# Four-layer graph attention: in the second layer, VectorE adds two of four weighted rows in every third group, and TensorE sums three

## The chip, the cores and the metric

The kernel runs on one core of a Trainium2 chip. The metric is the device time of one execution in microseconds, the median over several runs. In this text PE is TensorE, DVE is VectorE, ACT is ScalarE, POOL is GpSimd, and SP is the engine that issues plain DMAs.

## What is computed

There are 3327 nodes with 512 features each, and a sparse symmetric adjacency matrix (each node has some 17 neighbours on average, itself included). Four attention layers follow each other. Each one normalises the rows, applies a rectifier, projects with a 512 x 512 weight, and takes for every node the mean of its neighbours' projected rows, weighted by a softmax over the neighbours. The result is added to the input of the layer. The second layer has four heads of 128 features:

```python
def _L1_gnn_ref(H, A, W, a_l, a_r):
    mask = A + jnp.eye(n, dtype=A.dtype) > 0
    Wh = (H @ W).reshape(n, N_HEADS, D_K)
    sl = jnp.einsum('nhd,hd->nh', Wh, a_l)
    sr = jnp.einsum('nhd,hd->nh', Wh, a_r)
    e = jax.nn.leaky_relu(sl[:, :, None] + sr.T[None, :, :], negative_slope=NEG_SLOPE)
    e = jnp.where(mask[:, None, :], e, -jnp.inf)
    alpha = jnp.nan_to_num(jax.nn.softmax(e, axis=2), nan=0.0)
    out = jnp.einsum('nhm,mhd->nhd', alpha, Wh).reshape(n, OUT_DIM)
    return jax.nn.elu(out)
...
h = jnp.maximum(_layernorm(x, axis=-1), 0.0)
x = x + _L1_gnn_ref(h, adj, L1_gnn_W, L1_gnn_a_l, L1_gnn_a_r)
```

Layers 1 and 4 have eight heads, layer 3 has one. All arithmetic that matters here is in float32.

## The kernel before

The kernel first turns the adjacency matrix into lists of neighbours, ranks the nodes by their number of neighbours, and works on 26 tiles of 128 nodes in that order. `CAPS[t]` is the longest list in tile t: 36 for tile 0, 25 for tile 1, then falling to 11 for tile 25. Nodes with long lists (in the second layer, tile 0 alone; `DENSE`) are handled by dense products over the whole mask (class `Several`), spread over the same steps as the rest. This happens for each layer in turn; in code the second layer has `l == 1`.

For the other tiles (class `Tile`), the neighbours' rows are fetched in groups of four (`GROUP`). A tile with K neighbours has K/4 groups, rounded up, and the last group can be shorter. A group goes through these stages:

- `fetch`: POOL issues one indirect DMA for each of the four rows (L834). It takes 128 rows of the projected table from DRAM into one of seven buffers `g`. The first row of a tile is the nodes' own and comes by a plain DMA from SP (L865).
- `scored`: VectorE adds the two score terms and applies the leaky rectifier (z, L887 and L889), ScalarE takes the exponential into `pw` (L890).
- `group`: VectorE multiplies each of the four rows by its weights, head by head, into a buffer `m` (L916; three such buffers). TensorE then adds the rows up in a PSUM bank: each row is multiplied by the identity matrix and accumulated (L921), from the tile's first row to its last.

When a tile's last group is done, `finish` puts its epilogue in later steps: `divisors` and `means` on VectorE (L926 to L938), the ELU (`bent` on ScalarE at L944 and L946, `added` on VectorE at L952 and L958), then the variance (L966 and L969 on ScalarE, L974 and the root at L434 to L440 on VectorE), the transposes (L450), the projection for the next layer (L468), and the store of the projected rows (L475 on ScalarE, L992 on SP).

Everything is in program order: the outer loop runs over steps, one group each, and each engine executes its instructions in the order in which the loop writes them. In step s the order is: what is due "first" (a part of the dense work, transposes), then `scored` of group s + 1, what is due at "scored", then `group` of step s, then what is due "last". Tiles run from 25 down to 1.

Of the kernel before, what the change touches and what calls it, by code (L numbers as in the profile page):

```python
# [35 lines left out]
GROUP = 4  # L36
# [759 lines left out]
def tile_gat_lists(ctx: ExitStack, tc: tile.TileContext, x, adj, ws, avs, out, ident, half, slots, L, low, spare, tabx, tabs):  # L796
# [7 lines left out]
    nc = tc.nc  # L804
# [40 lines left out]
    class Tile:  # L845
# [51 lines left out]
        def group(self, i):  # L897


            H, K, wt = HEADS[self.l], CAPS[self.t], self.wt  # L900
            D = F // H
            k0, n, g = self.groups[i]
            if H == 1:
                for q in range(n):
                    v = g[:, q, :].rearrange("p (s m) -> p s m", s=2)[:, :, :F // 2]
                    acc = self.po.rearrange("p (s m) -> p s m", s=2)
                    w = wt[:, k0 + q, 0:1]
                    if k0 + q == 0:
                        nc.vector.tensor_scalar(acc, v, w, None, OP.mult)
                    else:  # L910
                        nc.vector.scalar_tensor_tensor(acc, v, w, acc, OP.mult, OP.add)  # L911
                return
            m = pools["m"].tile([P, GROUP, F], F32, name="m")
            for q in range(n):
                v = g[:, q, :].rearrange("p (s m) -> p s m", s=2)[:, :, :F // 2]
                nc.vector.tensor_tensor(m[:, q, :].rearrange("p (s h d) -> p s h d", s=2, d=D),  # L916
                                        v.rearrange("p s (h d) -> p s h d", d=D),
                                        wt[:, k0 + q, :H].rearrange("p (s h) -> p s h", s=2)
                                        .unsqueeze(3).to_broadcast([P, 2, H // 2, D]), OP.mult)
            for q in range(n):  # L920
                nc.tensor.matmul(self.po, ident, m[:, q, :], start=(k0 + q == 0), stop=(k0 + q == K - 1))  # L921

        def divisors(self):
            H, K = HEADS[self.l], CAPS[self.t]
# [420 lines left out]
    for l in range(NL):  # L1345
# [3 lines left out]
        with ExitStack() as c2:  # L1349
# [39 lines left out]
            for s in range(-1, at_end):  # L1389
# [10 lines left out]
                if 0 <= s < len(steps):  # L1400
                    tl, i = steps[s]
# [55 lines left out]
```

## Time and profile before

| | us |
|---|---|
| median of three runs without the profiler (2468.46 to 2473.81) | 2471.52 |
| the profiled execution's own time | 3002.17 |
| its span, first to last instruction | 3000.4 |

| stage of the profiled execution | from, to (us) | PE busy | DVE busy | ACT busy | POOL busy |
|---|---|---|---|---|---|
| lists and first projection | 0, 319 | 206.65 | 247.25 | 180.84 | 232.20 |
| layer 1 | 319, 1137 | 600.90 | 461.69 | 180.26 | 469.23 |
| layer 2 | 1137, 1850 | 552.88 | 439.62 | 197.21 | 369.40 |
| layer 3 | 1850, 2312 | 349.23 | 363.80 | 169.94 | 290.16 |
| layer 4 | 2312, 3000 | 530.86 | 398.97 | 185.64 | 388.29 |

The stages are cut where the first and last summing matmuls of a layer lie. A row of the profile names the line, the engine, the operation, output and inputs, the number of instructions, their busy time and the mean duration of one, then the idle time of that engine ahead of them and what ended it. The matmuls' durations overlap, so their sum isn't the time that the engine needs.

### The profile page before, as it was taken

The numbers are of one execution on the slowest core, as the hardware profiler recorded it, in microseconds if no ns is written. First come the engines' busy times: TensorE is split into PE (matmuls) and PEld (weight loads), VectorE is DVE, ScalarE is ACT, GpSimd is POOL, SyncE is SP. The second block draws the span as 40 slices with busy tenths as digits, with TensorE's granted clock in tenths as the row PEclk, the third lists the DMA queues.
The fourth block names the chain that finished last, engine by engine and source line by source line (L and its number), as shares of the span: only waits on it lengthen the run. The fifth ranks groups of instructions, "written<-read, shape, count | busy, mean of one in ns | idle before, by whom it ended". The sixth has DMA issues, their size and how long they took to land. (4 is left out here: it accounts for less than half of the span.)

```text
span 3000.4 us, 26820 instructions
## 1 busy us (share of the span) xinstructions
PE 2240.5 (75%) x6832; PEld 1225.4 (41%) x6832; DVE 1911.3 (64%) x5004; ACT 913.9 (30%) x2506; POOL 1749.3 (58%) x1739
## 2 busy tenths in 40 slices
PE   4777677777767756778778787679796677888787
PEld 2664243443334333444434344345354343444443
DVE  7887656655555545557665564697887456666655
ACT  5782122322221112323232222343333223332220
POOL 7894455565556646454556562676663556565654
PEclk9888888998899888889988888899898788898988
DMA  6885576786676677666766663787784667676664
GB/s 232 309 294 162 163 221 200 212 253 205 189 206 192 199 186 209 181 177 179 200 183 196 181 186 105 236 247 229 218 253 123 202 187 206 182 202 192 202 171 122
DMA packets 262490, 599.55 MB, mean 200 GB/s; under 512 B 103923, under 2 KB 121331, under 8 KB 257974
## 3 DMA queue, kind: packets, MB, share of 16 engines
q0 software_dynamic: 126128, 438.08, 49.7%
q1 hardware_dynamic: 132454, 152.86, 16.1%
q10 hardware_dynamic: 3744, 6.82, 0.7%
q8 instruction: 55, 0.90, 0.1%
q14 instruction: 109, 0.89, 0.1%
HBM read 547.96 MB, written 49.65 MB: 199 GB/s over the span
## 5 line engine op out<-in xcount | busy, mean ns | idle before, releaser
L921 PE MATMUL bank<-m,ident 128*128 128x512 f32 x2608 | 1328.8, 657 | 376.6 <-DVE m L916 218.1
L916 DVE TENSOR_TENSOR m<-g,pw 128x512 f32<-128x512 f32 x1304 | 811.1, 682 | 539.0 <-ACT pw L890 254.4
L834 POOL DMA_INDIRECT g<-tab,idxb x734 | 698.5, 952 | 482.2 <-issue 200.9
L921 PEld LDWEIGHTS bank<-m,ident 128*128 128x128 f32 x2608 | 528.0, 210 | 1038.3 <-issue 646.6
L468 PE MATMUL pv<-w,hT 128*128 128x264 f32 x1664 | 437.7, 418 | 80.0 <-ACT hT L457 45.5
L834 POOL DMA_INDIRECT g<-tabx,twiceb x342 | 324.2, 948 | 248.4 <-issue 153.7
L834 POOL DMA_INDIRECT g<-tab,idxa x297 | 283.0, 953 | 231.1 <-issue 95.6
L468 PEld LDWEIGHTS pv<-w,hT 128*128 128x128 f32 x1664 | 335.9, 206 | 182.5 <-ACT hT L457 52.3
L890 ACT ACTIVATE pw<-z 128x32 f32<-128x32 f32 (+4 forms) x362 | 69.1, 191 | 801.6 <-DVE z L889 442.5
L1146 PE MATMUL whole<-ve,em 128*128 128x512 f32 x468 | 230.1, 644 | 52.0 <-issue 21.8
L694 POOL TENSOR_TENSOR key<-a,keys 128x3328 int32<-128x3328 int32 (+1 forms) x29 | 189.4, 6534 | 16.2 <-DVE cand L703 12.6
L911 DVE SCALAR_TENSOR_TENSOR bank<-g,L,bank 128x512 f32<-128x512 f32 x243 | 183.3, 754 | 11.8 <-remote 3.9
L1146 PEld LDWEIGHTS whole<-ve,em 128*128 128x128 f32 x468 | 94.2, 207 | 164.7 <-issue 124.3
L834 POOL DMA_INDIRECT g<-tabx,twicea x99 | 94.4, 954 | 105.6 <-issue 55.5
L703 DVE MAX8 cand<-key 128x8 f32<-128x208 int32 x416 | 143.9, 364 | 0.1
L450 PE MATMUL pt<-ident,xn 128*128 128x128 f32 x416 | 71.4, 300 | 95.6 <-ACT xn L966 48.4
L475 ACT ACTIVATE v<-pv,rstd 128x528 f32<-128x528 f32 x78 | 54.1, 694 | 265.9 <-remote 118.6
L1271 ACT ACTIVATE spare<-room,low 128x64 f32<-128x64 f32 x208 | 57.9, 337 | 191.7 <-remote 82.2
L450 PEld LDWEIGHTS pt<-ident,xn 128*128 128x128 f32 x416 | 55.6, 155 | 137.8 <-ACT xn L966 54.9
L887 DVE TENSOR_TENSOR z<-g,pw 128x32 f32<-128x32 f32 (+4 forms) x362 | 63.1, 174 | 73.2 <-DMA g<-tab,idxa 43.3
L457 ACT ACTIVATE hT<-pt 128x512 f32<-128x512 f32 x104 | 61.4, 590 | 153.8 <-remote 85.1
L1260 ACT ACTIVATE r<-low,spare 128x256 f32<-128x256 f32 x208 | 98.9, 476 | 10.2 <-remote 2.3
(180 smaller groups left out, 2189.4 us busy)
## 6 DMA issues: line engine op xcount, KB each, us to landing
a<-in_adj SPq DMA_DIRECT2D x25, 1664.0 KB
tab<-v SPq DMA_DIRECT2D x78, 264.0 KB
ve<-tab SPq DMA_DIRECT2D x78, 264.0 KB
g<-tab SPq DMA_DIRECT2D x66, 264.0 KB
tabx<-vx SPq DMA_DIRECT2D x26, 528.0 KB
g<-tab,idxb POOLq DMA_INDIRECT x734
low<-tab SPq DMA_DIRECT2D x52, 132.0 KB
room<-tab SPq DMA_DIRECT2D x52, 132.0 KB
```

Source lines behind the costliest of these rows:

```text
L450: nc.tensor.transpose(pt[:, k, :], xn[:, k * P:(k + 1) * P], ident)
L468: nc.tensor.matmul(pv[:, s, :HF + 8], hT[:, k, :], W.w[:, k, s, :], start=(k == 0), stop=(k == KC - 1))
L694: nc.gpsimd.tensor_tensor(key[:, c:c + quarter], a[:, c:c + quarter], keys[:, c:c + quarter], OP.mult)
L703: nc.vector.max(cand[:, g * 8:(g + 1) * 8], key[:, g * SEG:(g + 1) * SEG])
L834: nc.gpsimd.indirect_dma_start(out=out_, out_offset=None, in_=table, in_offset=bass.IndirectOffsetOnAxis(ap=which, axis=0))
L887: nc.vector.tensor_tensor(z, g[:, :n, ROW - 8:ROW - 8 + H], self.s.unsqueeze(1).to_broadcast([P, n, H]), OP.add)
L890: nc.scalar.activation(self.wt[:, k0:k0 + n, :H], z, AF.Exp)
L911: nc.vector.scalar_tensor_tensor(acc, v, w, acc, OP.mult, OP.add)
L916: nc.vector.tensor_tensor(m[:, q, :].rearrange("p (s h d) -> p s h d", s=2, d=D), v.rearrange("p s (h d) -> p s h d", d=D), wt[:, k0 + q, ...
L921: nc.tensor.matmul(self.po, ident, m[:, q, :], start=(k0 + q == 0), stop=(k0 + q == K - 1))
L1146: nc.tensor.matmul(tl.po.rearrange("p (s m) -> p s m", s=2), e[:, q * P:(q + 1) * P], v.rearrange("p (s m) -> p s m", s=2)[:, :, :F // 2], ...
L1260: nc.scalar.activation(self.r[:, h, :], self.a[:, g, :], AF.Relu, bias=-1.0, scale=self.b[:, j, g:g + 1])
```

## The change

In the second layer, in a group of four rows whose number i in its tile is divisible by three, VectorE adds the second weighted row to the first in place, and TensorE leaves out the matmul of the second. The matmul of the first row then takes the sum of both. In all other groups nothing changes, nor does the order of the steps.

```diff
@@ def group(self, i):
+            pair = self.l == 1 and n == GROUP and i % 3 == 0
+            if pair:
+                nc.vector.tensor_add(m[:, 0, :], m[:, 0, :], m[:, 1, :])
             for q in range(n):
-                nc.tensor.matmul(self.po, ident, m[:, q, :], start=(k0 + q == 0), stop=(k0 + q == K - 1))
+                if not (pair and q == 1):
+                    nc.tensor.matmul(self.po, ident, m[:, q, :], start=(k0 + q == 0), stop=(k0 + q == K - 1))
```

The changed kernel has the same line numbers up to L919, and five more from L921 on.

## The prediction

> **What bounds the kernel now.** I looked first at the span and the time of the profiled execution: span 3000.4 us, time 3002.17 us, against a median of 2471.52 us without the profiler. The profiled execution is 531 us (21%) longer than the runs that count, so everything below is summed against 3002 us, and I have to ask for each stall whether it exists in the undisturbed runs. The split by stage (the busy time of each engine in windows cut where each layer's first and last `bank` matmuls lie) gives for the second layer:
>
> ```profile
> core 0: us, PE busy (x) PEld busy (x) DVE busy (x) ACT busy (x) POOL busy (x), PEclk, DMA share, GB/s
> ...
> 1137.00:1850.00 713.00, 552.88 (x1575) 291.33 (x1574) 439.62 (x1187) 197.21 (x594) 369.40 (x391) 0.89 0.62 178
> ```
>
> PE has 553 of 713 us, VectorE 440; no engine is full. The groups of lines in that window show the work:
>
> ```profile
> L921 PE MATMUL bank<-m,ident 128*128 128x512 f32 x855 | 431.4, 652 | 137.7 <-DVE m L916 115.9 <-issue 20.2 <-DVE z L889 1.1
> ...
> L916 DVE TENSOR_TENSOR m<-g,pw 128x512 f32<-128x512 f32 x423 | 263.1, 682 | 84.1 <-ACT pw L890 49.0 <-remote 17.4 <-issue 10.4
> ...
> L408 DVE TENSOR_TENSOR prod<-w,av 128x512 f32<-128x512 f32 x8 | 5.5, 688 | 0.0
> ```
>
> PE's idle time ahead of the summing matmul ends 116 us with the arrival of a product from VectorE. Why is the product late? The waits of VectorE in this window, longest first:
>
> ```profile
> DVE bank L952 <- ACT ex L946: 71.0, 10, 12.7
> DVE ve L974 <- ACT waste L969: 56.2, 16, 11.6
> DVE m L916 <- ACT pw L890: 49.0, 71, 6.7
> ```
>
> These are some ten microseconds at a time, about once in each tile; I counted 32 gaps over 0.8 us with 210 us in them, and 39 us of short round trips to ScalarE. In the list of waits ScalarE, which works in order, is stuck at the same moments on loads (L1271 <- remote, 53.8 us) while gathers fill the DMA queues. I take it that much of the 531 us that the profiler adds lies in such stalls. So the stretch that best resembles the undisturbed run is one without them, and the stage's end, where all gathers have landed:
>
> ```profile
> 1384.00:1428.00 44.00, 40.78 (x126) 22.38 (x126) 36.71 (x99) 18.09 (x60) 23.99 (x26) 0.96 0.65 187
> ...
> 1812.00:1837.00 25.00, 25.00 (x67) 12.56 (x66) 19.55 (x50) 5.21 (x13) 0.00 (x0) 0.93 0.10 33
> ```
>
> There PE is busy 93% and 100% of the time, VectorE 83% and 78%, and VectorE's remaining gaps are mostly the 0.25 to 0.31 us after each exponential. Over the stage VectorE needs 440 + 39 = 479 us in order. For PE, whose matmuls overlap (eight of L921 take 3.60 us in the timeline, so 0.43 us each and 0.86 us for a weighted row, which is two instructions), the sum is 431 rows x 0.86 = 371, the projection 25 x 3.72 = 93, the dense products 50 x 0.61 = 31, the transposes 25 x 0.60 = 15: 510 us at full clock. POOL's 391 gathers at 1.25 us from start to start are 489 us. Three engines within 7% of each other: none bounds the stage alone.
>
> **What the Trainium skill says.** "VectorE: DVE Perf Modes", section "The TRN2 errata", prices an fp32 tensor_tensor add at (N+151)/0.96 ns, 691 ns at N = 512; the trace agrees (L408, the same shape with both inputs in SBUF: 688 ns). "Perfetto Trace Analysis", section "Per-instruction lifecycle", says that TensorE's end times are estimates; hence I use the spacing 0.43 us and not the 652 ns of the row. "TensorE: Matmul & The Clock Gate", part 1, says the clock is full or half and falls after idle windows; the stage's mean is 0.89, and starts 0.85 us apart stand in the first layer at about 1016 us. "GPSIMD Engine Reference", section 1, says GpSimd's SBUF interfaces are contended by VectorE instructions with two SBUF inputs; the new add is one. No row of the trace before isolates this.
>
> **The change, part by part.** Tiles 1 to 25 of the second layer have 431 rows in 118 groups. A group with four rows and i of 0 or 3 qualifies (6 never has four rows): 25 first groups and 16 fourth ones, 41 in all.
>
> Removed on PE: 41 rows x 2 instructions x 0.43 us = 35.3 us at full clock, 39.6 us at the mean clock 0.89. No DMA, no other engine's instruction goes. The accumulation's first and last matmul stay (q = 0 and q = 3).
>
> Added on VectorE: 41 adds. Alone 0.69 us; in a run of like instructions they start 0.60 us apart (four products take 2.48 us), and one that waits for another starts at that one's end. 41 x 0.62 = 25.4 us taken, bounds 41 x 0.60 = 24.6 and 41 x 0.73 = 29.9. The order of instructions shows the add behind the fourth product, with a wait on VectorE's own earlier products. Queued behind it are the next instructions of the step: the scores z of the next group, or on i = 3 the variance chain (L974, L434 to L440). ScalarE's next exponential waits for z, and POOL's gathers wait for buffers that VectorE frees: each may move by 0.62 us. The release of the group's own gather buffer comes with the products and doesn't move.
>
> Moved: the matmul on q = 0. It now waits for the add. Before, it could start after the first product. In the timeline of tile 24, group 0:
>
> ```profile
> 1145.14 2.48 DVE L916 TENSOR_TENSOR m<-g,pw 128x512 f32<-128x512 f32 x4 [3.22 <-ACT low L1272]
> ...
> 1145.89 3.70 PE L921 MATMUL bank<-m,ident 128*128 128x512 f32 x8 [0.85 <-issue]
> ```
>
> PE starts 0.75 us after VectorE. With the add the products end at 1147.63, the add at about 1148.25, so PE starts at 1148.3 instead of 1145.9: 2.4 us later, with 0.86 us less to do. **Here PE is 1.56 us later after the change, not 0.86 us earlier.** The point from which a group gains is plain: PE has to be behind the end of the fourth product by 0.68 us anyway. I paired the starts of products and matmuls of all 118 groups in the timeline. Of the 41 affected, 27 have PE waiting for the first product (sum +42 us of PE lateness), 8 are in between (+5 us), and 6 are fully covered (6 x -0.86 = -5.2 us). Of the other 77 groups only 15 have PE waiting. The first group of a tile follows a short last group of the one before, and the fourth follows a stall, so the condition i % 3 == 0 picks the groups where PE is hungry. That lateness isn't all lost: it moves into PE's next idle time (160 us in the stage). It does mean that the 35 us saved fall mostly into idle time.
>
> The sum, against the profiled execution: of VectorE's 25.4 us a part is taken up by its idle time, 249 of 712 us or 35%, so 65% or 16.5 us stay; from this go the 5.2 us of the six covered groups: +11 us, 3013 us for a profiled execution. For the undisturbed median, which has fewer stalls, I carry the +11 us over: less idle to swallow the adds, but also more groups where PE is behind; I see no better split. 2471.5 + 11 = 2482 us. PE's clock and GpSimd's port I set at nothing: a gap of 2.4 us may cost a few matmuls at half clock, 41 x 0.86 at worst; the port could delay a gather by one add, 41 x 0.62 = 25 us at worst, covered as long as POOL stays ahead by its seven buffers.
>
> **Rivals.**
> *PE is the bound (faster).* For it: 25.00 of 25 us at the stage's end and 93% in the undisturbed stretch, and 510 us against 479. If PE lags by over 0.68 us at the affected groups in the undisturbed run, the saving counts up to 35 to 40 us. Against it: VectorE rises to 479 + 25 = 504 us, PE falls to 475, POOL stays at 489, so the largest of the three falls only by 6 us, and 27 of 41 groups find PE hungry. I give half of 35 us at most: 2454 to 2466, middle 2460.
> *No difference.* POOL and DMA set the pace (489 us of issue; POOL's wait of 131 us for freed buffers speaks against), both shifts vanish in stalls, or the two effects cancel: 2467 to 2476.
> *Slower by all of it.* VectorE is the bound and nothing hides the adds: 41 x 0.62 to 0.73, +25 to +30 us, 2497 to 2501; decisive if VectorE's gaps in the undisturbed run are only the short round trips.
> *The change doesn't do what it says.* The order of instructions shows 41 more on VectorE and 41 fewer matmul commands on PE, each recorded twice in a trace; I give this no chance.
>
> **How the numbers follow.** Some 0.2%, 5 us, is what a measurement of this kernel can tell from no change. Slower: 0.46 (0.36 partly hidden, 2477 to 2492; 0.10 in full). No difference: 0.20. Faster: 0.34. The range leaves out the full saving below and the upper end of the full cost: 2455 to 2498. The likeliest case alone is 2477 to 2492.
>
> **What would show it.** In the profile after: L921 (its matmul now L926) with 82 fewer, a new VectorE row L923 with 41 at about 0.69 us; the affected groups' first matmul starting 3.1 us behind the first product where PE was hungry; VectorE's busy time in the stage near 468 us, PE's near 515; the stage's length up by about ten. I am wrong if PE's wait for products in the stage doesn't grow, or if the covered groups are the majority.

## The result, and the profile after

The changed kernel takes 2512.6 us (median of 4 runs, 2510.77 to 2515.02) against 2470.99 us before: a ratio of 1.0168, interval 1.0155 to 1.018, or 41.6 us more. For 41 sums that is 1.01 us each, where the add alone lasts 0.68 us.

The first profile of the kernel before (span 3000.4 us) moved the same 599.55 MB at 200 instead of 243 GB/s, a condition that one later series met as well, so every ratio here is against the kernel before in the same series, and the profile before used from here on is a second one of the same code.

Span and clock of that second profile of the kernel before, and then the same of the changed kernel:

```profile
core 0: 2472.3 us, clock 0.942
```

```profile
core 0: 2512.3 us, clock 0.937
```

The spans differ by 40.0 us. The second layer's stage, from its first product to the end of its last summing matmul, is 528.3 us before and 570.3 us after: 42.0 us, which is everything. The busy times in that stage, in windows cut to it, of before (columns: window, its length, then busy time and number of instructions of PE, PEld, DVE, ACT and POOL, granted clock, DMA share, GB/s):

```profile
949.00:1478.00 529.00, 507.44 (x1574) 275.54 (x1574) 442.11 (x1183) 194.17 (x596) 375.42 (x396) 0.99 0.81 242
```

and of the changed kernel:

```profile
950.00:1521.00 571.00, 498.89 (x1492) 269.02 (x1492) 465.69 (x1225) 195.00 (x597) 383.14 (x397) 0.95 0.76 225
```

VectorE has 23.6 us more to do (the adds overlap with their neighbours, so this is less than the 28.0 us of their row below). PE has 82 matmul instructions less, yet its busy time falls by 8.5 us only: its clock was 0.99 and is 0.95. The groups of lines of the stage, before:

```profile
L921 PE MATMUL bank<-m,ident 128*128 128x512 f32 x862 | 393.2, 602 | 30.5 <-DVE m L916 30.2
...
L916 DVE TENSOR_TENSOR m<-g,pw 128x512 f32<-128x512 f32 x431 | 267.9, 681 | 32.5 <-ACT pw L890 31.2 <-PE whole L1294 0.7 <-PE bank L921 0.3
```

and after:

```profile
L926 PE MATMUL bank<-m,ident 128*128 128x512 f32 x780 | 382.0, 636 | 80.7 <-DVE m L923 67.5 <-DVE ve L979 8.4 <-DVE m L916 4.8
...
L923 DVE TENSOR_TENSOR m<-m 128x512 f32<-128x512 f32 x41 | 28.0, 683 | 0.0
```

PE's idle time ahead of the summing matmuls grew from 30.5 to 80.7 us, and 67.5 us of it end with the new add. In one group, tile 12's first, it looks as follows. Before, in order of time (start, length):

```profile
1193.47 2.48 DVE L916 TENSOR_TENSOR m<-g,pw 128x512 f32<-128x512 f32 x4 [0.31 <-ACT pw L890]
1194.21 3.70 PE L921 MATMUL bank<-m,ident 128*128 128x512 f32 x8 [1.04 <-DVE m L916]
```

and after:

```profile
1212.16 2.48 DVE L916 TENSOR_TENSOR m<-g,pw 128x512 f32<-128x512 f32 x4 [0.31 <-ACT pw L890]
1214.56 0.68 DVE L923 TENSOR_TENSOR m<-m 128x512 f32<-128x512 f32 x1
...
1215.30 4.54 PE L926 MATMUL bank<-m,ident 128*128 128x512 f32 x6 [3.44 <-DVE m L923]
```

PE starts 3.14 instead of 0.74 us behind the products, as the prediction worked out. But eight matmuls took 3.70 us and six take 4.54 us, since the clock drops behind the gap of 3.44 us: each matmul has one weight load, and the last three of these six start some 0.85 us apart, where 0.43 us is usual.

```profile
1216.26 0.33 PEld L926 LDWEIGHTS bank<-m,ident 128*128 128x128 f32 x1 [0.24 <-issue]
1217.12 0.33 PEld L926 LDWEIGHTS bank<-m,ident 128*128 128x128 f32 x1 [0.52 <-issue]
1217.97 0.33 PEld L926 LDWEIGHTS bank<-m,ident 128*128 128x128 f32 x1 [0.52 <-issue]
```

Of the 41 groups, 36 now start at the end of the add.

Who waits for a PE that is late? VectorE's waits in the stage, before (waiting instruction, what it waits for: total us, times, longest):

```profile
DVE m L916 <- ACT pw L890: 31.2, 114, 0.5
DVE ve L974 <- ACT waste L969: 14.7, 14, 2.4
DVE bank L952 <- ACT ex L946: 9.7, 14, 1.5
```

and after:

```profile
DVE m L916 <- ACT pw L890: 33.1, 112, 2.3
DVE bank L957 <- ACT ex L951: 23.3, 15, 4.1
DVE ve L979 <- ACT waste L974: 16.8, 7, 3.9
```

ScalarE's waits for PE, before:

```profile
ACT v L475 <- PE pv L468: 18.4, 8, 9.8
ACT hT L457 <- PE pt L450: 11.9, 10, 2.6
ACT low L1271 <- PE whole L1294: 2.1, 4, 0.6
```

and after:

```profile
ACT v L475 <- PE pv L468: 24.6, 11, 9.1
ACT hT L457 <- PE pt L450: 20.0, 12, 4.0
ACT low L1276 <- PE whole L1299: 12.0, 5, 3.2
```

ScalarE waits 57 us for PE instead of 32, and VectorE's wait for the ELU's exponential rises by 13.6 us. One such chain in the timeline of the changed kernel:

```profile
1194.82 0.69 DVE L943 TENSOR_TENSOR bank<-bank,den 128x512 f32<-128x512 f32 x1
...
1195.92 3.72 PE L468 MATMUL pv<-w,hT 128*128 128x264 f32 x16
...
1199.68 0.70 ACT L475 ACTIVATE v<-pv,rstd 128x528 f32<-128x528 f32 x1 [2.35 <-PE pv L468]
...
1200.28 0.59 ACT L949 ACTIVATE neg<-bank 128x512 f32<-128x512 f32 x1
...
1200.90 0.63 ACT L951 ACTIVATE ex<-neg 128x512 f32<-128x512 f32 x1
...
1201.56 0.69 DVE L957 SCALAR_TENSOR_TENSOR bank<-ex,bank 128x512 f32<-128x512 f32 x1 [1.72 <-ACT ex L951]
```

The projection on PE ends late; ScalarE stands 2.35 us at L475, which scales an older tile's projection; the ELU of the next tile (L949, L951), which needs nothing of that projection, queues behind it, although its input had been ready since the end of L943 at 1195.51; VectorE stands 1.72 us.

### The profile page after: what moved, and what is told of

Same layout as the page of the kernel before. It is cut to its first block, busy times and chain, and to the rows that moved or that the text cites. A ratio compares the mean times of both kernels' runs of the same rounds, so it can differ in the third digit from the quotient of the medians.

```text
span 2512.3 us, 26697 instructions
## 1 busy us (share of the span) xinstructions
PE 2069.9 (82%) x6750; PEld 1155.1 (46%) x6750; DVE 1941.2 (77%) x5045; ACT 910.6 (36%) x2506; POOL 1756.1 (70%) x1739
## 2 busy tenths in 40 slices
DMA packets 262490, 599.55 MB, mean 239 GB/s; under 512 B 103923, under 2 KB 121331, under 8 KB 257974
## 5 line engine op out<-in xcount | busy, mean ns | idle before, releaser
L926 PE MATMUL bank<-m,ident 128*128 128x512 f32 x2526 | 1189.3, 617 | 181.4 <-DVE m L916 105.2
L926 PEld LDWEIGHTS bank<-m,ident 128*128 128x128 f32 x2526 | 473.8, 196 | 756.2 <-issue 369.8
L468 PE MATMUL pv<-w,hT 128*128 128x264 f32 x1664 | 432.4, 414 | 73.2 <-ACT hT L457 48.0
L1117 ACT ACTIVATE r<-low,mc,b 128x384 f32<-128x384 f32 x78 | 52.6, 675 | 148.8 <-DVE em L1124 129.1
L889 DVE SCALAR_TENSOR_TENSOR z<-z 128x32 f32<-128x32 f32 (+5 forms) x434 | 82.9, 191 | 15.1 <-DVE z L887 0.2
L475 ACT ACTIVATE v<-pv,rstd 128x528 f32<-128x528 f32 x78 | 54.0, 692 | 97.6 <-PE pv L468 74.8
```

The costliest lines, as they stand in the source:

```text
L468: nc.tensor.matmul(pv[:, s, :HF + 8], hT[:, k, :], W.w[:, k, s, :], start=(k == 0), stop=(k == KC - 1))
L889: nc.vector.scalar_tensor_tensor(z, z, SLOPE, z, OP.mult, OP.max)
```

## The experiments

Times are against the kernel before in the same series: the ratio's excess over 1, times the median of before. Idle time of VectorE is summed over gaps of more than 0.15 us. The letters A, B and C stand for the three explanations that the expectations of add_aside set against each other: the adds' own time, the late start of PE, and GpSimd held up. Each profile is of one execution.

**The kernel before, once more** (base_again, no edit).

> The kernel before, profiled once more, since the first profile of it was 21% longer than its runs and the profile after was not. If the long stalls of the first profile belong to that one execution, this span lies near 2470 us, VectorE's idle time in the second layer's stage falls from 249 us to about 50 to 80 us, and the stage from 712 us to about 530 us (570 us after, less the 41.6 us). If the profiler disturbs the kernel before as such, the span is again near 3000 us.

It took 2474.0 us under the profiler, span 2472.3 us. So neither the profiler as such nor the code makes the gaps of ten microseconds that the prediction saw; they belong to the condition of that execution. VectorE's idle time in the stage is 64.7 us, not 249. PE waits for the first product in 18 of the 41 groups instead of 27: 17 of the 25 first groups, but 1 of the 16 fourth ones.

**The add alone** (add_aside). TensorE sums all four rows; VectorE's sum goes into a tile that nobody reads. The edit, against the kernel before:

```diff
+            pair = self.l == 1 and n == GROUP and i % 3 == 0
+            if pair:
+                aside = pools["q"].tile([P, F], F32, name="aside")
+                nc.vector.tensor_add(aside, m[:, 0, :], m[:, 1, :])
...
```

> The 41 adds are made, but into a tile that nobody reads, and TensorE sums all four rows as before: nothing of PE's work or order changes. Theory A (VectorE's serial order is the bound, the adds' own 0.6 to 0.7 us each are what is paid): +25 to +30 us against before. Theory B (what is paid is the first matmul's wait for the add, and PE's lateness behind it): +0 to +10 us. Theory C (the add's two SBUF inputs hold up GpSimd's descriptor work): as A or more, with gathers of over 1.1 us beside the adds and gaps of VectorE ahead of z that end with a gather.

+12.9 us (1.0052, 1.0035 to 1.0069), between A and B, in neither's range: VectorE's time is paid, but not all of it. The stage in its profile:

```profile
950.00:1494.50 544.50, 509.99 (x1574) 275.47 (x1574) 465.92 (x1226) 193.79 (x597) 381.51 (x397) 0.99 0.79 236
```

VectorE is busy 23.8 us longer, and its idle time falls from 64.7 to 56.1 us, so 8.6 us are swallowed and the stage is 15.2 us longer.

**The saving alone** (three_only). The second row's matmul is left out without an add, so its sum lacks those rows. The edit, against the changed kernel:

```diff
-            if pair:
-                nc.vector.tensor_add(m[:, 0, :], m[:, 0, :], m[:, 1, :])
```

> TensorE leaves out the second row's matmul in the 41 groups, without an add: the sum lacks those rows. It shows what PE's saving of 35 us is worth alone. Theory A: little, 0 to -10 us, since PE isn't the bound. Theory B: -5 to -20 us, since PE's lateness counts. If PE is the bound: -25 to -40 us.

-1.2 us (0.9995, 0.9986 to 1.0004): in these 41 groups, 35 us of PE's work are worth nothing that can be measured, although PE was busy 507 of 529 us before. The stage in its profile:

```profile
953.00:1482.50 529.50, 490.27 (x1492) 261.61 (x1492) 440.90 (x1183) 193.73 (x596) 375.57 (x396) 0.97 0.81 242
```

PE's busy time falls by 17.2 us only, at a clock of 0.97. It was tried in these groups alone, where PE often waits for VectorE anyway; what less work would be worth in the others isn't shown.

**The sum last** (sum_last). PE takes rows 2 and 3 first, and the sum last. Of the edit, against the changed kernel, the new lines:

```diff
...
+            turns = [2, 3, 0] if pair else range(n)
+            for a, q in enumerate(turns):
+                nc.tensor.matmul(self.po, ident, m[:, q, :], start=(i == 0 and a == 0),
+                                 stop=(k0 + n == K and a == len(turns) - 1))
```

> The change, but TensorE takes rows 2 and 3 of an affected group first and the sum last, so that its first matmul waits for the third product and not for the add. Theory A: within 8 us of the changed kernel (+34 to +42 us against before). Theory B: most of the loss goes, +0 to +15 us against before.

+19.1 us (1.0077, 1.0051 to 1.0103). With the same instructions on every engine and only PE's order turned, over half of the 41.6 us goes, more than A allowed and less than B. VectorE's idle time in the stage is 58.7 us, against 83.5 us in the changed kernel. So the late start (B) is the larger part; of the 19.1 us that stay, the adds (A) explain 12.9.

**The late start alone** (late_start). The kernel before, no add, all four matmuls, the fourth row's first.

```diff
-            for q in range(n):
-                nc.tensor.matmul(self.po, ident, m[:, q, :], start=(k0 + q == 0), stop=(k0 + q == K - 1))
+            late = self.l == 1 and n == GROUP and i % 3 == 0
+            turns = [3, 0, 1, 2] if late else range(n)
...
```

> The kernel before, without any add: in the same 41 groups TensorE takes the fourth product first and then the other three, so that it waits for the last product instead of the first one. PE's work and VectorE's work are those of before; only PE's start moves, by up to 3 x 0.60 = 1.8 us where it was hungry. Theory B (a late start of PE is paid, since ScalarE's work on PE's results stands ahead of the ELU and the variance that VectorE waits for): +15 to +30 us against before. If lateness costs only together with the adds (VectorE then has no slack left): +0 to +8 us.

+28.7 us (1.0116, 1.0083 to 1.0149). Its profile:

```profile
952.50:1511.50 559.00, 515.98 (x1574) 279.34 (x1574) 441.80 (x1183) 196.11 (x597) 376.63 (x396) 0.97 0.77 229
```

VectorE's busy time is that of before, the stage is 30.2 us longer, and all of it is VectorE's idle time (94.9 instead of 64.7 us). PE's busy time is 8.5 us longer for the same instructions, at a clock of 0.97 instead of 0.99; so a slower clock behind the new gaps is a part of what a late start costs here. In three_only the clock was 0.97 too and nothing was lost, but there PE had less to do.

The add and the late start by themselves make 12.9 + 28.7 = 41.6 us, which is the loss of the change. The sum is that exact by chance: the intervals are 4 and 8 us to either side, and the two delays are alike but not the same (here PE starts up to 1.8 us later with four rows to sum, in the change 2.4 us later with three).

**The place** (first_only: i == 0; third_only: i == 2). The edit of first_only, against the changed kernel:

```diff
-            pair = self.l == 1 and n == GROUP and i % 3 == 0
+            pair = self.l == 1 and n == GROUP and i == 0
```

> The change in the first group of each tile alone (i = 0, 25 groups). In the new profile of before 17 of these 25 groups have PE waiting for the first product. Theory B: 25 adds cost 12.9 x 25/41 = 8 us by themselves, and the late start comes on top: +18 to +30 us against before. Theory A alone: +8 us.

> The change in the third group of each tile alone (i = 2, 24 groups of four rows). In the new profile of before PE is on average 1.77 us behind the last product there, so the add is over before PE could start. Theory B: no late start, the adds' own cost only, 12.9 x 24/41 = 8 us, +4 to +10 us against before. If the place doesn't matter: the changed kernel's 41.6 x 24/41 = 24 us.

First groups: +33.6 us (1.0136, 1.0112 to 1.0161) for 25 sums, 1.34 us each, and somewhat more than was expected. Third groups: +8.2 us (1.0033, 1.0021 to 1.0044) for 24 sums, 0.34 us each, the rate of add_aside (12.9/41 = 0.31). Where PE is behind anyway, no more than the add is seen to be paid. The cost of the change lies mostly in the tiles' first groups.

**The add early** (early_add): behind the second product instead of the fourth.

```diff
...
+                if pair and q == 1:
+                    nc.vector.tensor_add(m[:, 0, :], m[:, 0, :], m[:, 1, :])
...
```

> The change with the add right behind the second product and ahead of the third and fourth: the same instructions on every engine, PE may start 1.2 us earlier than in the changed kernel, with a short dependence of the add on the product ahead of it. Theory B: between sum_last and the changed kernel, +20 to +32 us against before. Theory A: as the changed kernel or 1 to 3 us more.

+22.5 us (1.0091, 1.0066 to 1.0115): in the middle one of the first groups PE starts 2.07 us behind the first product instead of 3.14, and this takes 19 us off, without any work saved.

**The way back to VectorE** (after_rows: the changed kernel; before_rows: the kernel before). In the second layer, L475 moves from the place "scored" to the end of its step.

```diff
-                                    (b + 3, "last", self.project), (b + 5 - (HEADS[self.l] == 1), "scored", self.rows),
+                                    (b + 3, "last", self.project),
+                                     (b + 5 - (HEADS[self.l] == 1), "last" if self.l == 1 else "scored", self.rows),
```

> The changed kernel with one more edit: in the second layer, ScalarE's scaling of the projected rows (L475, which waits for PE's projection) is put at the end of its step instead of ahead of the next exponential and, in tiles of five groups, ahead of the ELU. If PE's lateness reaches VectorE through that instruction (ScalarE works in order; its waits for PE grew from 32 to 57 us), most of the 28.7 us that the late start cost comes back: +14 to +25 us against before. If it reaches VectorE by another way (the transposes, the dense products, the end of a tile): +34 us or more.

> The control: the same move of L475 in the kernel before. There the waits of VectorE for ScalarE's ELU are 9.7 us, so it can give back little: -8 to +3 us against before. A larger gain would say that the gain in the other kernel has nothing to do with the pair sums.

The changed kernel with the move: +19.0 us (1.0077, 1.0063 to 1.0091), 22.6 us less than without. The kernel before with it: -6.2 us (0.9975, 0.9966 to 0.9983). So between the two kernels 25.2 us of loss are left instead of 41.6, and 16.4 us come back through the place of L475 alone. In after_rows VectorE waits for the ELU 9.9 us instead of 23.3. ScalarE's waits at L457 and the dense products stay at 24.2 and 12.5 us.

**The rest of the way** (late_rows, late_rows_2: late_start with the same move).

> late_start (no add, PE takes the fourth product first in the 41 groups) with L475 moved to the end of its step as in after_rows. If the cost of a late start goes through L475 alone, the 28.7 us shrink to what the move gives by itself, -6 to +5 us against before. If the other two waits of ScalarE for PE (the transposes L457 and the dense products' L1271) carry a part, which in after_rows still were 24 and 12 us, +6 to +15 us stay.

In that series the kernel before took 2967.22 us, and late_rows 2968.54 (1.0007, 0.9986 to 1.0027): the late start and the move together change nothing there that can be measured. What each does there by itself isn't shown, and the result can't be set beside late_start. The same code once more, in another series:

> late_rows once more: in its first runs the kernel before itself took 2967 us instead of 2471 us (as in the very first profile), so that they can't be set beside late_start. If the kernel before takes some 2471 us this time: -6 to +5 us against before when L475 carries the whole cost of the late start, +6 to +15 us when ScalarE's other waits for PE carry a part. If it takes some 2970 us again: within 6 us of it, as the first time.

+13.6 us (1.0055, 1.0041 to 1.0068) with before at 2471.76 us. The move takes 15.1 of the 28.7 us off, but it takes 6.2 us off the kernel before as well. With the move in both, the late start still costs 13.6 + 6.2 = 19.8 us, so L475 carries 8.9 us of it, about a third; the intervals of the three runs together make 9 us to either side, as much as the figure itself. The profiles say the same: the stage is 30.2 us longer with a late start without the move, and 20.1 us (544.1 against 524.0) with it. Where the rest goes is what ScalarE's waits in this run suggest:

```profile
ACT hT L457 <- PE pt L450: 33.1, 19, 3.8
ACT v L475 <- PE pv L468: 22.2, 9, 9.8
ACT low L1276 <- PE whole L1299: 15.4, 12, 4.1
```

L457 and the dense products' copy have 48.5 us here, against 14.0 in the kernel before and 19.5 in before_rows. That they carry the rest was not tried by moving them.

**GpSimd's SBUF interface** (aside_psum: add_aside's adds replaced by products with the weights in PSUM, one SBUF input).

> add_aside with its 41 adds replaced by products of the same size whose second input is the weight in PSUM, so that they have one SBUF input like the kernel's other products; all four matmuls stay. In add_aside 23 gathers took over 1.05 us, against 2 in before. If the contention for GpSimd's SBUF interface is part of the 12.9 us: +4 to +9 us and no long gathers. If only VectorE's own time counts: +12 to +15 us, with few long gathers all the same.

+10.1 us (1.0041, 1.0028 to 1.0055), between the two ranges expected, and 2 gathers over 1.05 us instead of 23. The longer gathers come from the second SBUF input, then; whether they cost time is not decided, since the intervals of 10.1 and 12.9 us overlap.

**The opposite** (act_row): ScalarE makes the fourth product of each tile's third group, with weights from a small exponential of its own.

```diff
...
+                if self.l == 1 and n == GROUP and i == 2 and q == 3:
+                    for h in range(H):
+                        nc.scalar.activation(m[:, q, h * D:(h + 1) * D], v[:, h // 2, h % 2 * D:(h % 2 + 1) * D],
+                                             AF.Copy, scale=self.w3[:, h:h + 1])
+                    continue
```

> The opposite of the change, on the kernel before: in the third group of each tile ScalarE makes the fourth product, head by head (four instructions, and a small exponential into SBUF for the weights), and VectorE one product less: 24 x 0.6 = 14 us less on VectorE, some 38 us more on ScalarE, PE as before. If VectorE's serial time is what bounds the stage: -5 to -12 us against before. If it is not, or ScalarE's in-order work holds the ELU up: 0 to +10 us.

-4.9 us (0.998, 0.9971 to 0.999), at the edge of what was expected if VectorE's time is the bound. VectorE has 14 us less to do, and a third of it comes back in the time. Work taken off VectorE pays where work taken off PE did not, though in other groups.

**Both moves** (both_moves, both_moves_2: before_rows and act_row).

> before_rows and act_row together: L475 at the end of its step, and the fourth product of each tile's third group on ScalarE. The first gave -6 us, the second -5 us. If both shorten VectorE's chain, one by its waits and one by its work, they add up: -8 to -13 us against before. If ScalarE's longer work in the third group takes back what the move gives: -3 to -7 us.

> both_moves once more, for the same reason. If the kernel before takes some 2471 us: -8 to -13 us against before when the two moves add up, -3 to -7 us when they don't. If it takes some 2970 us again: -3 to -12 us.

First -6.8 us (0.9977, 0.9959 to 0.9996) with before at 2967.22 us; then -8.7 us (0.9965, 0.9951 to 0.9978), 2464.8 us with before at 2471.76. It beats both kernels. Its interval overlaps that of before_rows, so whether the two add up in full isn't shown.

## Why the prediction was wrong

The direction and the mechanism's first half were right: more on VectorE, a later first matmul, and a saving that lands where PE has nothing to win. The size, 11 us, was a quarter of 41.6 us, and the range ended at 2498.

- **"That lateness isn't all lost: it moves into PE's next idle time".** This step failed. It asked who waits on PE's own queue, and set what PE's lateness does to others at nothing. late_start measures it: 28.7 us. ScalarE executes in order, and its work on PE's results stands ahead of what VectorE waits for. For one instruction this is shown: moving L475 takes 16.4 of the 41.6 us off, beyond what the move gives the kernel before. For ScalarE's other reads of PE's results it is read from the waits alone.
- **The adds, 16.5 us.** add_aside measured 12.9 us. The add's duration, 0.68 us, and the 2.4 us of delay in a hungry group were right. That the term came near is luck in part: it let VectorE's idle share of the first profile, 35%, swallow the adds, and with the share of the second, 64.7 of 528.3 us, the same rule gives 22 us.
- **The covered groups, -5.2 us.** three_only gives -1.2 us for all 41 groups, not clear of nothing. PE's "25.00 of 25" and 93% were read as a sign that PE might be the bound; three_only and act_row speak for VectorE's pace with PE close behind.
- **The count of hungry groups.** It came from a profile with long stalls. In the second profile the fourth groups are nearly all out of it, and first_only shows that the first groups carry 33.6 of the 41.6 us.
- **"PE's clock and GpSimd's port I set at nothing".** The clock fell from 0.99 to 0.95 in the stage. The 35 us of saved matmuls became 8.5 us of busy time. What the clock alone costs was not separated. At GpSimd, add_aside has 23 gathers over 1.05 us and aside_psum 2; a cost in time isn't shown (12.9 against 10.1 us).
- **The 531 us as the profiler's.** base_again refutes it. The stall-free stretch was nevertheless close to the undisturbed stage: PE was busy 93% and VectorE 83% of it, against 96% and 84% in the second profile.

Of the rivals, "slower by all of it" allowed 25 to 30 us for adds that nothing hides. It went in the right direction for the wrong reason: the adds by themselves cost 12.9 us.

## What to carry to other kernels

Before moving work from one engine to another, leave the work out on the first engine and see whether the time falls: PE was busy 96% of the stage, and 35 us less of its work, in the groups in question, gave nothing. Count a delayed start as a cost of its own, and follow it through the in-order queues of the engines that read the delayed results, to the instructions that stand behind those reads. If a sum in place must be made, let the consumer take what it doesn't touch first, and put it where the consumer is behind: the same add cost 1.34 us in a tile's first group and 0.34 us in its third.

## What the runs showed of the hardware

A gap of 3.44 us ahead of six matmuls was followed by 4.54 us for them, where eight had taken 3.70 us behind a gap of 1.04 us. In the changed kernel's stage, summing matmuls start behind a gap of over 0.3 us 37 times. In all 12 cases with a gap of 2.56 us or more, some of the next matmuls start 0.85 us apart instead of 0.43; with gaps of 1.93 to 2.44 us that is so in 3 of 8 cases, and directly behind the 17 shorter gaps in none. So it was at waits of some 2 us that a late start began to cost PE clock here.

Indirect gathers issued by GpSimd, usually 0.95 us each, took over 1.05 us 23 times in the stage when VectorE made 41 adds with both inputs in SBUF (add_aside), and 2 times when those instructions had one input in PSUM (aside_psum).
